# Moving a 32-byte constant to the front of its pool in a two-layer graph kernel on one NeuronCore

## The chip, the cores and the metric

The kernel runs on one core of one Trainium2 chip. The metric is device time in microseconds for one execution of the whole program. Before the change, three runs gave 1968.35, 1971.6 and 1975.02 us; the median is 1971.6 us.

## The reference, cut to what matters

The input is `x` with 128 batches of 128 rows by 512 features, and one 128x128 adjacency matrix `adj`. Two residual layers are applied, each followed by a layer norm.

```
# layer 0
A = adj @ x ;  C = adj @ x + b
y = max over features of relu(A_j + (C - A)_i)      # with equal weights this is relu(max_j A_j + b), one number per row
x = layernorm(x + y)
# layer 1: masked attention with 8 heads of 64
q, k, v = x @ w_qkv
p = softmax(where(adj == 0, -inf, q k^T / 8))
o = (p v) @ w_proj + b_proj
x = layernorm(x + o + layernorm(o) * gamma + beta)
```

## The kernel before, in words

The 128 batches are taken in 32 groups of four (`G = 4`). Within one group the matrix unit, TensorE, has these pieces of work:

- `conv` (line 186): `adj @ x` for one batch, in float32, with `adjT` as the stationary operand (the weights that are loaded into the array) and the batch's `xt` as the moving operand (the one that streams past). It feeds layer 0.
- `dense` (lines 342, 343 and 350): the q, k and v products of layer 1. To be fast and still exact enough, both factors are split into a high part, a low part and a difference, all kept in the type `fp32r`: `x_h`, `x_l`, `x_d` for the activations of a group and `w_h`, `w_l`, `w_d` for the weights. A product takes twelve matmuls of 128x128 against 512 columns: four slices of the inner dimension, each with the pairs of the high parts (342) and the low parts (343), and then four of the differences (350). The eight q and k products of a group have `w_*` stationary and `x_*` moving. The four v products have `x_*` stationary and `w_*` moving.
- `scores` (line 397) and `attend` (line 477): q times k, and v times the softmax weights, in float32, sixteen pairs of small matmuls a batch.
- `po` (function `project`, also lines 342, 343 and 350): the output projection, again twelve `fp32r` matmuls, with `p_h`, `p_l`, `p_d` moving and the split attention output `oh`, `ol`, `od` stationary. For the last eight batches (120 to 127) the split attention output is not put into `oh`, `ol`, `od`: the function `heads` writes it into slices of `w_h`, `w_l`, `w_d`, whose q and k columns are no longer needed by then. In the profile these projections are the ones that read `p_h,w_h` and so on.

The other engines feed this. VectorE (DVE) masks the scores, takes row maxima, scales the softmax weights and makes the low parts (lines 294 and 296). ScalarE (ACT) takes exponentials, norms and the high parts (line 303). GpSimd (POOL) makes the differences `x_d` and `od` (line 308) and prepares the residual `xb` (lines 500, 501 and 518; line 501 adds `beta_sb`). SyncE (SP) issues the transfers in a single queue, in order. Two of them are transposes through DRAM: the normalised batch (`xplanes` to `rowsx`, line 279, then `xT`, line 283) and the softmax weights (`planes` to `rows`, line 450, then `eT`, line 455).

The order on each engine is written out by a plan: a table of offsets `O` places each step relative to the matrix unit's estimated timeline, the steps are sorted by that place, and the order is then fixed (`tc.manual_schedule`).

SBUF memory is given out by pools, one after the other, in the order in which the pools are opened and, within a pool, in the order in which tiles are asked for; each tile takes a multiple of 32 bytes of every partition. The pool `const` comes first. It holds, in this order, `b0_sb` (4 bytes, padded to 32), `ident`, `adjT` and `mask` (512 bytes each), the six weight tensors `w_h` to `p_d`, `gamma_sb`, `bias_sb`, `beta_sb` (2,048 bytes each), the small constant `mhalf` (16 bytes, padded to 32; the exponent -0.5 that POOL uses at lines 241 and 536), and `square`. All large tensors of the pool have sizes that are multiples of 512 bytes. So the distance of a tensor from a multiple of 512 bytes (its address modulo 512) is set by what small tiles stand ahead of it:

| tensors | address modulo 512, before |
|---|---|
| `b0_sb` | 128 |
| `ident`, `adjT`, `mask`, `w_h` ... `p_d`, `gamma_sb`, `bias_sb`, `beta_sb`, `mhalf` | 160 |
| `square` and every large tile of the later pools: `xt`, `x_h`, `x_l`, `x_d`, `v`, `qkT`, `e`, `eT`, `o`, `xb`, `oh`, `ol`, `od` | 192 |

Of the kernel before, what the change touches and what calls it, by code (L numbers as in the profile page):

```python
# [8 lines left out]
FP = mybir.dt.float32  # L9
# [17 lines left out]
def tile_adj_resnorm_d2(  # L27
# [39 lines left out]
    P = 128  # L67
    assert T == P and D == 512 and B % 4 == 0
    G = 4
# [6 lines left out]
    const = ctx.enter_context(tc.tile_pool(name="const", bufs=1))  # L76
# [15 lines left out]
        xs[b] = xt  # L92


    adj_sb = work.tile([P, D], FP, tag="xh", name="adj_sb")[:, :P]
    nc.scalar.dma_start(adj_sb, adj)
    b0_sb = const.tile([P, 1], FP, name="b0_sb")
# [67 lines left out]
    gamma_sb = const.tile([P, D], FP, name="gamma_sb")  # L165
    bias_sb = const.tile([P, D], FP, name="bias_sb")
    beta_sb = const.tile([P, D], FP, name="beta_sb")
    mhalf = const.tile([P, G], FP, name="mhalf")
    nc.vector.memset(mhalf, -0.5)
    square = const.tile([P, D], mybir.dt.bfloat16, name="square")  # L170

# [727 lines left out]
```

## Time and profile before

| what | value |
|---|---|
| median of three runs | 1971.6 us (1968.35 to 1975.02) |
| profiled execution, span from the first to the last instruction | 1967.2 us |
| TensorE (PE) busy | 1872.0 us, 95% of the span |
| VectorE (DVE) busy | 1648.1 us, 84% |
| ScalarE (ACT) busy | 1547.6 us, 79% |
| GpSimd (POOL) busy | 1246.0 us, 63% |
| mean granted TensorE clock | 0.989 |

The profile shows one execution. Its page gives the span and no separate total for that execution; the span is 4.4 us under the median of the three runs, which also hold what lies around the first and the last instruction. A steady group takes about 58.9 us. A busy matrix unit in this profile is not one at its peak: the time of one matmul is best read from the distance between the starts of neighbours, since the ends are modelled.

### The profile page before, as it was taken

How to read it: one execution, taken by the hardware profiler on the slowest of the kernel's cores; microseconds unless marked ns; L12 is line 12 of the kernel's file. 1: busy time of each engine (PE TensorE's matmuls, PEld its weight loads, DVE VectorE, ACT ScalarE, POOL GpSimd, SP SyncE). 2: the span in 40 equal slices, each digit the busy share in tenths (PEclk: the TensorE clock that was granted, in tenths of full speed). 3: DMA queues.
4: the chain of work that ended last, by engine and by line, in shares of the span. 5: the costliest groups of instructions: out<-in, count | busy, mean ns of one | idle time of the engine just before them, and what ended most of it. 6: DMA issues, size and time to landing. Idle time of an engine off the chain costs nothing.

```text
span 1967.2 us, 33044 instructions
## 1 busy us (share of the span) xinstructions
PE 1872.0 (95%) x10569; PEld 1438.1 (73%) x10569; DVE 1648.1 (84%) x2585; ACT 1547.6 (79%) x3926; POOL 1246.0 (63%) x1935
## 2 busy tenths in 40 slices
PE   7799999999999999999999999999999999999995
PEld 4677777777777777777777777777777777777774
DVE  7778888888888888888888888888888888888875
ACT  4688878788878788878788878788878788878764
POOL 3256666666666666666666666666667666667667
PEclk9899999999999999999999999999999999999997
DMA  4366565666565666555666555766555666555641
GB/s 130 102 156 163 152 157 147 175 172 164 152 159 147 172 172 162 153 158 149 173 172 166 151 156 147 175 171 166 151 160 145 173 172 164 153 156 146 154 114 52
DMA packets 486141, 302.92 MB, mean 154 GB/s; under 512 B 399440, under 2 KB 403664, under 8 KB 485968
## 3 DMA queue, kind: packets, MB, share of 16 engines
q1 hardware_dynamic: 485104, 299.70, 57.2%
q8 instruction: 84, 1.38, 0.3%
q10 hardware_dynamic: 864, 1.12, 0.2%
q14 instruction: 89, 0.73, 0.1%
HBM read 72.16 MB, written 131.07 MB: 103 GB/s over the span
## 4 chain that ended last, share of the span: by engine, by line
PE 70%; POOL 11%; DVE 9%; issue 5%; ACT 3%; DMA 3%; SPq 0%; POOLq 0%; ACTq 0%; DVEq 0%
POOL x_d L308 5%; PE psc L397 5%; PE pav L477 5%; PE pa L186 3%; POOL od L308 2%; DMA eT<-rows 2%; DVE x_l L296 1%; DVE v L381 1%; POOL sum L536 1%; DVE xh L294 1%; ACT oh L303 1%; DVE o L523 1%; DVE o L548 1%; DVE o L509 1%; ACT x_h L303 1%
## 5 line engine op out<-in xcount | busy, mean ns | idle before, releaser
L431 ACT ACTIVATE e<-e,nmax 128x128 f32<-128x128 f32 x1016 | 393.1, 389 | 62.5 <-DVE nmax L422 62.5
L446 ACT COPY planes<-e 128x2048 uint16<-128x2048 uint16 x124 | 234.7, 1893 | 21.6 <-DVE e L440 21.5
L529 ACT ACTIVATE square<-o,sum 128x512 bf16<-128x512 f32 x256 | 183.1, 715 | 63.8 <-DVE o L523 62.8
L535 POOL TENSOR_SCALAR sum<-sum 128x1 f32<-128x1 f32 (+1 forms) x287 | 58.3, 203 | 269.8 <-ACT square L529 256.6
L501 POOL TENSOR_TENSOR xb<-xb,beta_sb 128x512 f32<-128x512 f32 x128 | 210.6, 1646 | 10.7
L308 POOL TENSOR_TENSOR x_d<-x_h,x_l 128x512 fp32r<-128x512 f32 x97 | 125.7, 1310 | 134.6 <-DVE x_l L296 74.9
L536 POOL TENSOR_TENSOR sum<-sum,mhalf 128x1 f32<-128x1 f32 (+1 forms) x287 | 181.1, 631 | 23.9
L431 ACT ACTIVATION_READ_ACCUMULATOR e<-e,nmax 128x1 f32 x1016 | 190.9, 188 | 0.0
L518 POOL TENSOR_TENSOR xb<-xb,o 128x512 f32<-128x512 f32 x125 | 164.6, 1317 | 4.9
L440 DVE TENSOR_TENSOR e<-e,sums 128x1024 f32<-128x1024 f32 x128 | 162.3, 1268 | 4.4
L548 DVE SCALAR_TENSOR_TENSOR o<-o,sum,gamma_sb 128x512 f32<-128x512 f32 x128 | 99.3, 776 | 76.5 <-POOL xb L518 72.9
L413 DVE SCALAR_TENSOR_TENSOR e<-psc,mask 128x1024 f32<-128x1024 f32 x127 | 151.8, 1216 | 3.3 <-ACT planes L446 2.7
L422 DVE TENSOR_REDUCE nmax<-e 128x8 f32<-128x1024 f32 x127 | 153.5, 1209 | 0.1
L477 PE MATMUL pav<-eT,v 128*64 128x128 f32 x2048 | 140.1, 280 | 11.4 <-DMA eT<-rows 5.4
L556 ACT ACTIVATE o<-o,sum 128x512 f32<-128x512 f32 x128 | 103.1, 807 | 54.6 <-POOL sum L544 54.6
L397 PE MATMUL psc<-qkT 64*128 64x128 f32 x2048 | 141.8, 284 | 2.5 <-DVE qkT L381 2.5
L500 POOL TENSOR_SCALAR xb<-xb,sum 128x512 f32<-128x512 f32 x128 | 120.8, 944 | 35.3 <-DMA xb<-in_x_dram 33.9
L397 PEld LDWEIGHTS psc<-qkT 64*128 64x128 f32 x2048 | 123.4, 189 | 25.9 <-issue 21.4
L259 ACT ACTIVATE xt<-xt,sum 128x512 f32<-128x512 f32 x127 | 102.4, 806 | 46.3 <-POOL sum L250 45.2
L477 PEld LDWEIGHTS pav<-eT,v 128*64 128x64 f32 x2048 | 110.8, 137 | 37.3 <-issue 15.4
L277 ACT COPY xplanes<-xt 128x1024 uint16<-128x1024 uint16 x124 | 129.7, 1046 | 5.1 <-DMA rowsx<-xplanes 1.2
L186 PE MATMUL pa<-xt,adjT 128*128 128x512 f32 x256 | 123.6, 607 | 6.9 <-ACT v L325 3.5
(4668 smaller groups left out, 5606.3 us busy)
## 6 DMA issues: line engine op xcount, KB each, us to landing
rows<-planes SPq DMA_DIRECT2D x124, 512.0 KB, 3.3
xt<-in_x_dram SPq DMA_DIRECT2D x128, 256.0 KB, 3.0
xb<-in_x_dram SPq DMA_DIRECT2D x128, 256.0 KB, 3.0
out_dram<-o SPq DMA_DIRECT2D x128, 256.0 KB, 2.8
rowsx<-xplanes SPq DMA_DIRECT2D x124, 256.0 KB, 2.4
wraw<-in_L_gnn_w_qkv_dram SPq DMA_DIRECT2D x8, 256.0 KB, 2.9
xT<-rowsx SPq DMA_TRANSPOSE x124, 3.6
eT<-rows SPq DMA_TRANSPOSE x124, 4.7
```

Source lines behind the costliest of these rows:

```text
L186: nc.tensor.matmul(pa[b], adjT, xs[b], start=True, stop=True)
L308: engine.tensor_tensor(fd, fh.bitcast(FP), fl.bitcast(FP), op=ALU.subtract)
L397: nc.tensor.matmul(psc[:, s, hp, :], qkT[hs, hp, i, :], qkT[hs, KC + hp, i, :], start=not with_mask, stop=not with_mask or hp == HP - 1,)
L422: nc.vector.tensor_reduce(nmax, src, AX.X, ALU.max, negate=True)
L431: nc.scalar.activation(e[:, j, :], src[:, j, :], AF.Exp, bias=nmax[:, j : j + 1], scale=1.0 if src is e else scale, accum_out=sums[:, j : ...
L440: nc.vector.tensor_tensor(e, e, sums[:, :, None].to_broadcast([P, H, P]), op=ALU.mult)
L446: nc.scalar.copy(planes, e.rearrange("p h m -> p (h m)").bitcast(U16).rearrange("p (m s) -> p s m", s=2),)
L477: nc.tensor.matmul(pavs[b][s * HD : (s + 1) * HD, hp, :], v[:, h * HD : (h + 1) * HD], eT[:, s * HP + hp, :], start=True, stop=True,)
L501: nc.gpsimd.tensor_tensor(xbs[b], xbs[b], beta_sb, op=ALU.add)
L518: engine.tensor_tensor(xbs[b], xbs[b], os[b], op=ALU.add)
L529: nc.scalar.activation(square, x, AF.Square, bias=s[:, 0:1], scale=-float(D), accum_out=s[:, 1:2],)
L536: nc.gpsimd.tensor_tensor(s, s, mhalf[:, :n], op=ALU.pow)
```

## The change

One line is moved and reworded. The tile `mhalf` is asked for at the start of the pool `const`, ahead of `b0_sb`, instead of after `beta_sb`. It is asked for with eight columns, of which a view takes the first four, so it takes 32 bytes in either place. The instructions that fill it (a memset on VectorE and a copy on ScalarE) stay where they were.

```diff
+    mhalf = const.tile([P, 8], FP, name="mhalf")[:, :G]
     adj_sb = work.tile([P, D], FP, tag="xh", name="adj_sb")[:, :P]
     nc.scalar.dma_start(adj_sb, adj)
     b0_sb = const.tile([P, 1], FP, name="b0_sb")
 ...
     beta_sb = const.tile([P, D], FP, name="beta_sb")
-    mhalf = const.tile([P, G], FP, name="mhalf")
     nc.vector.memset(mhalf, -0.5)
```

Every engine has the same instructions in the same order as before. What moves is memory: `mhalf` takes the place at 128, and `b0_sb`, `ident`, `adjT`, `mask`, the six weight tensors, `gamma_sb`, `bias_sb` and `beta_sb` lie 32 bytes further on. `square` and all later tiles keep their addresses. So the tensors at 160 modulo 512 go to 192, where the activations and split operands already are.

## The prediction

> **What bounds the kernel now.** I read the page first: busy shares, the slices over time and the chain that ended last.
>
> ```profile
> span 1967.2 us, 33044 instructions
> ...
> PE 1872.0 (95%) x10569; PEld 1438.1 (73%) x10569; DVE 1648.1 (84%) x2585; ACT 1547.6 (79%) x3926; POOL 1246.0 (63%) x1935
> ...
> PE   7799999999999999999999999999999999999995
> ...
> PE 70%; POOL 11%; DVE 9%; issue 5%; ACT 3%; DMA 3%; SPq 0%; POOLq 0%; ACTq 0%; DVEq 0%
> ```
>
> The matrix unit is busy in nine tenths or more of nearly every slice and holds 70% of the chain, so a change in the time of one matmul can move the end. No other engine is at its limit, but all of them touch the chain.
>
> Next I looked at what the change touches on the matrix unit. The fp32r products of q, k, v and of the projection have one operand in `w_*` or `p_*` (160 modulo 512) and the other in `x_*` or `o*` (192). The last eight batches are an exception that the kernel before holds by itself: there both operands lie in `p_*` and `w_*`, so both at 160. The timeline of PE (start, busy us, line, operands) has the two kinds side by side:
>
> ```profile
> 1892.13 0.40 PE L342 MATMUL pm_(31, 1)_19611<-w_h,x_h 128*128 128x512 f32 x1
> ...
> 1893.99 1.10 PE L350 MATMUL pd_(31, 1)_19612<-w_d,x_d 128*128 128x512 f32 x4
> 1894.93 0.39 PE L342 MATMUL pm_('o', 120)_19626<-p_h,w_h 128*128 128x512 f32 x1
> ...
> 1896.74 1.07 PE L350 MATMUL pd_('o', 120)_19627<-p_d,w_d 128*128 128x512 f32 x4
> ...
> 1950.87 0.39 PE L342 MATMUL pp_('o', 126)_20088<-p_h,w_h 128*128 128x512 f32 x1
> ...
> 1952.68 1.07 PE L350 MATMUL pp_('o', 126)_20088<-p_d,w_d 128*128 128x512 f32 x4
> ```
>
> Eight matmuls lie between a first start and its line 350. Operands at unlike distances: 1893.99 - 1892.13 = 1.86 us, 232.5 ns each; with the next four, 1894.93 - 1892.13 = 2.80 us, 233.3 ns each over twelve. Like distances, immediately afterwards: 1896.74 - 1894.93 = 1.81 us, 226 ns each, and again 1.81 us at 1950.87. Instruction, shape and clock are the same, and the other engines' work is that of the same microseconds. Start by start, the unlike kind alternates between 231 and 235 ns, the like kind between 226 and 227.
>
> Last, the chain of waits over one steady group (start, us, what), to see which matmuls lie on it:
>
> ```profile
> 1023.38 0.25 PE pm_(16, 3)_10517 L343
> 1023.62 0.02 issue
> 1023.64 2.55 POOL x_d L308 x2
> ...
> 1029.56 1.30 POOL x_d L308
> 1030.86 1.42 POOL od L308
> 1032.28 0.04 issue
> 1032.32 1.20 PE pd_('o', 63)_10606 L350 x4
> ```
>
> From 1023.6 to 1032.3 the chain runs through POOL, while the matrix unit does the projection of batch 62, two convs and most of batch 63, and then waits 1.0 us for `od`. Everything else in the group, 1000.0 to 1058.9, is matmul after matmul.
>
> [...]
>
> **The change part by part.** It removes and adds no instruction, transfer or wait and moves no queue: the memset and the copy that fill `mhalf` keep their places. What it moves is the second operand.
>
> Number of matmuls: lines 342, 343 and 350 have 2,040 each, 6,120 in all. The projections of batches 120 to 127 (8 x 12 = 96) already have like distances, before and after. So 6,024 go from unlike to like.
>
> Price of one: 233.3 - 226.6 = 6.7 ns in a settled stream. But a like stream is not always settled from its first matmul. Batch 120 is; batches 121, 123 and 127 need six to ten matmuls after a pause at some 231 ns, and batch 124, which is broken up by a wait, does not settle. A steady group has 16 products of 12, which makes 192 fp32r matmuls, in about six streams, each begun after small matmuls or a wait. Eight slow ones each are 48 that win about 2 ns, and 144 win 6.7: 0.10 + 0.96 = 1.06 us a group, 5.5 ns a matmul. All 6,024 settled would be 40 us of PE time over the kernel; at 5.5 ns it is 33 us.
>
> What lies on the path: in the group shown, 12 matmuls of batch 62 and 8 of batch 63 lie beside POOL's stretch, so 172 of 192 are on the chain. The sum over the chain's pieces on these three lines is 1,141 us, or about 4,890 matmuls of 233.3 ns. They bound the gain: 4,890 x 6.7 = 33 us if all settle, 27 us at 5.5 ns. No faster matmul can bring more unless it settles below 226.
>
> What is late next: the softmax weights of the fourth batch of a group.
>
> ```profile
> 1011.42 0.34 SPq L279 DMA_DIRECT2D rowsx<-xplanes  x1
> 1011.86 2.13 SPq L455 DMA_TRANSPOSE eT<-rows  x1
> ...
> eT<-rows SPq DMA_TRANSPOSE x124, 4.7
> ```
>
> The queue's timeline and the page's transfer list: issued at 1011.86 behind `rowsx`, which waits for ScalarE's `xplanes` (line 277), and landed some 4.7 us later, at about 1016.5. The attend of that batch starts at 1016.56. Eleven times in the kernel PE is seen idle for it, 5.4 us in all. So the two v products and two projections ahead of it, 48 matmuls, run beside an equally long path through ScalarE, and what they win is lost in that wait unless ScalarE's work has come forward too. That leaves 172 - 48 = 124 matmuls a group: 124 x 5.5 = 0.68 us, times 31 groups, 21 us. With the 48 counted it is 29 us. I take 21, because the landing is that close in every group.
>
> Other engines: VectorE, ScalarE and POOL read `mask`, `gamma_sb`, `bias_sb` and `beta_sb` at the new place. I cost this at nothing. POOL's line 501 (`xb` at 192 with `beta_sb` at 160) has a mean of 1,646 ns against 1,317 for line 518 with both at 192, which could look like placement. But single ones of line 501 take 1.30 us (at 1899.57 in the chain), as line 518 does[...]. From both sides: if all of the difference were placement, POOL would gain 128 x 0.33 = 42 us of busy time, of which the chain holds six pieces of line 501, so 2 us; a loss is limited likewise.
>
> Sum: the span of 1967.2 becomes about 1946; against the median of the runs, 4.4 us above that span, 1971.6 - 21 = 1950.6, said as 1951.
>
> **The rivals.**
> 1. The gain is swallowed: each wait for `eT` and `od` grows by what PE wins. For it: `eT` lands as it is needed. Against: the chain goes through that transfer only eleven times, and the 72 matmuls of six q and k products in a row have no such partner. It would give 1961 to 1971.
> 2. The change doesn't do what it says: the quick projections are quick because both operands sit at 160, or because of which tensors they are, and 192 with 192 is like any other pair. Against: five of the projections reach 226 to 227 with weights at different multiples of 512. It gives 1971.6.
> 3. Slower: at a common distance of 192 the weight load and the moving read get into each other's way in every fp32r matmul. Place: the same 4,890 on the chain; price: as much as the gain, 6.7 ns, so 1971.6 + 33 = 2004; it decides from 1.2 ns a matmul (4,890 x 1.2 = 5.9 us). Against: the float32 scores have both operands in `qkT`, at 192, and the prologue's v products have both at 192 and take 429 ns an instruction, as the conv with unlike operands does.
> 4. More than forecast: all streams settle and ScalarE's path comes forward with them, 1971.6 - 33 = 1938, or lower if 192 is better than 160.
>
> **How the numbers follow.** The forecast, 14 to 34 us less, has 0.66; a larger gain 0.05; rival 1 has 0.17, most of it still over the bound; rival 2 has 0.05, rival 3 0.07. A measurement of this kernel can tell about 0.3%, 5.9 us, from no change. So faster has 0.84, same 0.09, slower 0.07. The range of 1937 to 1967 takes the settled bound at its low end and the weaker part of rival 1 at its high end.
>
> **What would show it.** Right: twelve fp32r matmuls of q, k and v in 2.72 to 2.77 us where there were 2.80, steps of 226 to 227 ns in the long q and k stretch, conv and scores unchanged, a steady group near 58.2 us, and longer waits of the fourth attend for `eT`. Wrong: steps that remain at 231 and 235 (rival 2) or go above (rival 3); or steps of 227 with a group of 58.9 us (rival 1).

## The result and the profile after

The changed kernel takes 1975.5 us (median of four runs, 1971.05 to 1979.84) against 1970.3 us for the kernel before beside it: a ratio of 1.0029 with a 95% interval of 1.0007 to 1.0051. It is no faster, but slower by some 5 us. The forecast of 1951 us, with a range of 1937 to 1967, was wrong.

The page of the changed kernel, for the execution of 1971.05 us:

```profile
span 1969.2 us, 33044 instructions
...
PE 1844.8 (94%) x10569; PEld 1438.0 (73%) x10569; DVE 1671.3 (85%) x2585; ACT 1550.6 (79%) x3926; POOL 1273.3 (65%) x1935
...
PE   7799999999999999999999999999999999999995
...
PE 59%; POOL 14%; DVE 9%; ACT 7%; issue 5%; DMA 5%; POOLq 0%; ACTq 0%; SPq 0%; DVEq 0%
```

PE works 27.2 us less than before (1872.0 - 1844.8) in a span that is 2 us longer, and its share of the chain falls from 70% to 59%. Two other engines, which execute the same instructions in the same order, are busier: VectorE by 23 us, POOL by 27 us. The granted clock is the same (0.988 after, 0.989 before).

The matmuls did what was forecast. The timeline of PE has three streams of twelve, one after the other:

```profile
1005.85 0.39 PE L342 MATMUL pm_('o', 60)_10338<-p_h,oh 128*128 128x512 f32 x1
...
1008.57 0.39 PE L342 MATMUL pm_(16, 1)_10370<-w_h,x_h 128*128 128x512 f32 x1
...
1011.29 0.39 PE L342 MATMUL pm_('o', 61)_10405<-p_h,oh 128*128 128x512 f32 x1
```

Twelve take 2.72 us, 227 ns each, where they took 2.80 us. Over the kernel the mean distance of neighbouring starts (pauses of 250 ns and more left out) went from 233.3 to 227.8 ns for q and k, and from 233.2 to 228.5 ns for v and the projections. Yet the median period of a steady group is 58.92 us, where it was 58.90. What PE won reappears as idle time ahead of the attend. The waits of PE (total us, times, longest us), where before had 5.4, 11 and 0.9:

```profile
PE pav L477 <- DMA eT<-rows: 28.7, 26, 2.6
```

The tempting reading is that the transfer of `eT` was tied with PE all along and has swallowed the gain. The other half of the profile speaks against stopping there. These are groups of instructions on the page (busy us, mean ns, idle before):

```profile
L518 POOL TENSOR_TENSOR xb<-xb,o 128x512 f32<-128x512 f32 x125 | 175.2, 1401 | 4.9
...
L523 DVE SCALAR_TENSOR_TENSOR o<-o,sum,xb 128x512 f32<-128x512 f32 x128 | 132.5, 1035 | 10.8 <-POOL sum L536 0.9
```

The same groups before, from the list of all groups:

```profile
L518 POOL TENSOR_TENSOR xb<-xb,o 128x512 f32<-128x512 f32 x125 | 164.6, 1317 | 4.9
...
L523 DVE SCALAR_TENSOR_TENSOR o<-o,sum,xb 128x512 f32<-128x512 f32 x128 | 112.6, 880 | 10.8 <-POOL sum L536 0.9 <-POOL sum L541 0.5
```

The timelines show where the difference comes from. First the kernel before, VectorE and POOL between 954 and 963 us, in a steady group:

```profile
954.67 0.69 DVE L509 SCALAR_TENSOR_TENSOR o<-pm_('o', 57)_9783,bias_sb 128x512 f32<-128x512 f32 x1 [0.98 <-PE pm_('o', 57)_9783 L343]
...
957.33 0.19 POOL L535 TENSOR_SCALAR sum<-sum 128x1 f32<-128x1 f32 x1 [0.76 <-ACT square L529]
...
958.27 1.51 POOL L301 TENSOR_SCALAR x_h<-xh 128x512 fp32r<-128x512 f32 x1
...
958.58 1.39 DVE L440 TENSOR_TENSOR e<-e,sums 128x1024 f32<-128x1024 f32 x1
959.87 1.30 POOL L518 TENSOR_TENSOR xb<-xb,o 128x512 f32<-128x512 f32 x1
...
962.13 0.75 DVE L523 SCALAR_TENSOR_TENSOR o<-o,sum,xb 128x512 f32<-128x512 f32 x1
```

Then the changed kernel, the same instructions of the same group:

```profile
954.40 0.69 DVE L509 SCALAR_TENSOR_TENSOR o<-pm_('o', 57)_9783,bias_sb 128x512 f32<-128x512 f32 x1 [0.84 <-PE pm_('o', 57)_9783 L343]
...
957.76 0.19 POOL L535 TENSOR_SCALAR sum<-sum 128x1 f32<-128x1 f32 x1 [1.33 <-ACT square L529]
...
958.46 1.23 DVE L440 TENSOR_TENSOR e<-e,sums 128x1024 f32<-128x1024 f32 x1
958.70 2.35 POOL L301 TENSOR_SCALAR x_h<-xh 128x512 fp32r<-128x512 f32 x1
...
961.13 1.76 POOL L518 TENSOR_TENSOR xb<-xb,o 128x512 f32<-128x512 f32 x1
961.85 1.59 DVE L523 SCALAR_TENSOR_TENSOR o<-o,sum,xb 128x512 f32<-128x512 f32 x1
```

Before, POOL starts its line 301 at 958.27, 0.31 us ahead of VectorE's line 440, both go on nearly undisturbed (1.51 and 1.39 us; in the group at 132.09 us, where line 301 starts 0.56 us ahead, 1.51 and 1.23), and POOL is through with line 518 at 961.17, before VectorE comes to line 523. After, line 440 starts first. The matmuls hand VectorE its input 0.27 us earlier (its line 509 starts at 954.40 instead of 954.67), while POOL is later: it waits until 957.76 instead of 957.33 for ScalarE's `square`, which stands in a backlog that ran 0.43 us later from its first copy on (line 277 at 951.87 instead of 951.44). Set against line 509, this first copy has moved by 0.70 us: it starts 2.53 us ahead of it instead of 3.23. Line 301 now takes 2.35 us, line 518 slides behind it, and line 523 meets line 518 and takes 1.59 us instead of 0.75. I call this the **meeting**. Of 26 steady groups it is there in all 26 after the change (line 523 takes over 1.2 us), and in 3 before.

From the start of line 509 (projection of a group's second batch) to the end of the fourth batch's line 413, VectorE needs 11.03 us before and 11.85 us after (medians over the groups; the idle time in it is 0.32 us in both). This is **VectorE's stretch** below. What follows is 0.8 us later for it, counted from line 509: `od` starts 8.97 us behind it instead of 8.14, POOL's `x_d` 10.89 instead of 10.07. That the delay goes on from there through ScalarE's backlog and `rowsx` in SP's queue to `eT` is argued from what depends on what; where it costs time is for the experiments to show.

In the two timelines, which pass starts first decides what VectorE loses. With POOL's line 301 ahead it is 0.16 us, on line 440 (1.39 us against 1.23). With line 440 ahead, line 301 takes 2.35 us instead of 1.51, and VectorE loses 0.84 us later, on line 523, which starts 0.72 us after line 518 (1.59 against 0.75). That passes of the two engines lengthen each other is measured; what they contend for is not shown.

### The profile page after: what moved, and what is told of

It reads as the page before. It is cut to its first block, busy times and chain, and to the rows that moved or that the text cites. A ratio compares the mean times of both kernels' runs of the same rounds, so it can differ in the third digit from the quotient of the medians.

```text
span 1969.2 us, 33044 instructions
## 1 busy us (share of the span) xinstructions
PE 1844.8 (94%) x10569; PEld 1438.0 (73%) x10569; DVE 1671.3 (85%) x2585; ACT 1550.6 (79%) x3926; POOL 1273.3 (65%) x1935
## 4 chain that ended last, share of the span: by engine, by line
PE 59%; POOL 14%; DVE 9%; ACT 7%; issue 5%; DMA 5%; POOLq 0%; ACTq 0%; SPq 0%; DVEq 0%
POOL x_d L308 5%; PE pav L477 4%; PE psc L397 4%; DMA eT<-rows 3%; PE pa L186 2%; POOL od L308 2%; ACT e L431 2%; POOL sum L536 2%; POOL xb L501 1%; DVE x_l L296 1%; DVE v L381 1%; DVE xh L294 1%; POOL xb L518 1%; POOL xb L500 1%; DVE o L523 1%
## 5 line engine op out<-in xcount | busy, mean ns | idle before, releaser
L518 POOL TENSOR_TENSOR xb<-xb,o 128x512 f32<-128x512 f32 x125 | 175.2, 1401 | 4.9
L440 DVE TENSOR_TENSOR e<-e,sums 128x1024 f32<-128x1024 f32 x128 | 157.7, 1232 | 4.4
L523 DVE SCALAR_TENSOR_TENSOR o<-o,sum,xb 128x512 f32<-128x512 f32 x128 | 132.5, 1035 | 10.8 <-POOL sum L536 0.9
```

The source lines that it names most:

```text
L440: nc.vector.tensor_tensor(e, e, sums[:, :, None].to_broadcast([P, H, P]), op=ALU.mult)
L518: engine.tensor_tensor(xbs[b], xbs[b], os[b], op=ALU.add)
L523: nc.vector.scalar_tensor_tensor(os[b], in0, scalar, in1, op0=ALU.mult, op1=ALU.add, accum_out=s[:, 0:1],)
```

## The experiments

Eighteen runs. The expectations name their theories themselves. In short, the theories are: the late `eT` in SP's queue eats the gain; the new place of `mask`, `gamma_sb`, `bias_sb` and `beta_sb` costs another engine time; PE and a second loop through POOL, ScalarE and SP are tied; and the meeting of VectorE and POOL. Every ratio is to the kernel before, on the same chip. A group is the median period over 26 steady groups of the profiled run.

### Getting `eT` out of SP's queue

The order on SP is set by due times. An early due time puts `eT` ahead of both `rowsx` transfers:

```diff
-'softmax': {'cross': [-11.04, -10.0, -15.2, -5.92],
+'softmax': {'cross': [-11.04, -10.0, -15.2, -40.0],
```

`b_early` is this in the kernel before, `a_early` in the changed one.

> The kernel before with one entry of the plan changed: the transfer of the softmax weights (eT) of the fourth batch of each group stands earlier in SP's queue, ahead of two rowsx transfers. Theory 1 (two loops of equal length, 58.9 us a group: one of matmuls, one through POOL, VectorE, ScalarE and SP that ends in this eT): the matmul loop is as long as before, so 1964 to 1972 us, and the idle time of PE ahead of attend for eT falls from 5.4 us to under 2. Theory 2 (the moved vectors slow VectorE and POOL): says nothing of this run beyond the same.

> The changed kernel with the same entry of the plan: eT of the fourth batch earlier in SP's queue. Theory 1: the wait of 28.7 us for eT goes to under 5, the 27 us of shorter matmuls show, and the time is 1945 to 1958 us, 14 us or more under the kernel before with the same entry. Theory 2 (the new place of mask, gamma, beta and bias slows VectorE and POOL and so sets the end): 1968 to 1976 us, no better than the changed kernel.

Measured: 2001.3 us (ratio 1.0152, 1.0126 to 1.0177) and 2000.1 us (1.0141, 1.0114 to 1.0168), a group of 59.9 and 59.8 us. The wait for `eT` is gone, but both times lie far above what every theory gave: this edit has a cost of its own. With it PE waits for `v` instead, probably because `rowsx` and the `xT` behind it, on which `v` depends, now come late. The waits of PE in `a_early`:

```profile
PE pav L477 <- ACT v L377: 17.1, 22, 1.8
```

Besides, the meeting is present in both (line 523 at 1.58 us), in the kernel before too. So the pair tells nothing of the gain. A milder due time puts `eT` ahead of one `rowsx` only, into a gap of SP's queue:

```diff
-'softmax': {'cross': [-11.04, -10.0, -15.2, -5.92],
+'softmax': {'cross': [-11.04, -10.0, -15.2, -8.5],
```

`a_c85` is this in the changed kernel, `b_c85` in the kernel before.

> The changed kernel with the eT of the fourth batch ahead of only one rowsx transfer, in a gap of 3.1 us that SP's queue has there. Theory 1 (the end is set by a loop without fp32r matmuls, which closes through this eT): the wait of 28.7 us for eT goes to under 6, no other transfer is held up by more than 1 us, and the gain of the matmuls shows: 1945 to 1962 us. Theory 2 (the new place of mask, gamma, beta and bias slows VectorE and POOL): 1968 to 1976 us. Theory 3 (several loops of nearly the same length, so that taking one away brings the next): 1960 to 1972 us with another wait of 15 us or more on PE.

> The kernel before with the same entry of the plan. Theory 1: the matmul loop is the only one left, 58.8 us a group: 1962 to 1971 us, with under 2 us of waits for eT. Theory 3: as much or slower, 1966 to 1976 us.

Measured: 1971.9 us (0.9998, 0.9989 to 1.0006) and 1969.5 us (0.9983, 0.9975 to 0.9992). In `a_c85` PE no longer waits for `eT`, and nothing is won: a group still takes 58.94 us. The wait moved to the first matmul of a projection. PE's timeline of `a_c85`, with the idle time ahead and its releaser in brackets:

```profile
971.02 0.50 PE L342 MATMUL pp_('o', 58)_9921<-p_h,oh 128*128 128x512 f32 x1 [1.29 <-DVE e L413]
```

The idle time of PE ahead of a projection that ends with VectorE's line 413, the end of VectorE's stretch, rose from 6.1 us in the changed kernel to 39.6 (between 120 and 1880 us; in `b_c85` it is 14.9). So the late `eT` was where most of the loss showed, not where it arose. The time alone would also fit the theory of the vectors' new place; the next pair tests that.

### The place of the vectors against the place of the weights

`w_only` has the six weight tensors alone at 192 (the three vectors and `mhalf` are asked for ahead of `w_h`), `v_only` has `ident`, `adjT`, `mask` and the vectors at 192 and the weights at 160.

```diff
 # w_only: ahead of w_h
+    gamma_sb = const.tile([P, D], FP, name="gamma_sb")
+    bias_sb = const.tile([P, D], FP, name="bias_sb")
+    beta_sb = const.tile([P, D], FP, name="beta_sb")
+    mhalf = const.tile([P, G], FP, name="mhalf")
```

```diff
 # v_only: the weights w_h ... p_d, then mhalf, ahead of ident
+    mhalf = const.tile([P, G], FP, name="mhalf")
     ident = const.tile([P, P], FP, name="ident")
```

> The six weight tensors alone at 192 modulo 512; ident, adjT, mask, gamma, bias and beta stay at 160. Theory 1: like the changed kernel, matmuls of 227 to 228 ns, 25 us or more of waits for eT, 1968 to 1977 us. Theory 2: matmuls of 227 to 228 ns, and the time 1940 to 1958 us, since the vectors have their old place.

> The other half alone: ident, adjT, mask, gamma, bias and beta at 192, the weight tensors at 160. Theory 1: like the kernel before, matmuls of 233 ns, VectorE's line of o<-o,sum,xb at 880 ns as before, 1966 to 1974 us. Theory 2: matmuls of 233 ns, VectorE's o<-o,sum,xb at 1,035 ns as in the changed kernel, and over 1980 us.

Measured: `w_only` 1979.5 us (1.0027, 1.0010 to 1.0044; 2.5 us above what theory 1 gave), matmuls at 227.8 to 228.4 ns, meeting present (stretch 11.86 us). `v_only` 1974.2 us (1.0005, 0.9996 to 1.0014), matmuls at 233.2 ns, no meeting (11.03 us). The place of the vectors is out as a cause: the faster matmuls bring the meeting with them.

### POOL with less to do

`b_nobeta` and `a_nobeta` leave out line 501 (`beta_sb` is not added to the residual).

```diff
-        nc.gpsimd.tensor_tensor(xbs[b], xbs[b], beta_sb, op=ALU.add)
```

> The kernel before without line 501: beta (zeros here) is not added to the residual, which takes 128 instructions of 1.65 us off POOL. Theory 1: the loop through POOL gets some 3 us a group shorter, the matmul loop stays 58.8 us, so the time falls by little: 1960 to 1970 us. Theory 2: the same.

> The changed kernel without line 501 (beta, zeros here, is not added). Theory 1: with the loop through POOL shorter, the matmul loop with its 5.5 ns less a matmul sets the end: 1940 to 1956 us, 14 us or more under the kernel before without that line, and the idle time of PE for eT is under 8 us. Theory 2: the two kernels without that line differ by less than 6 us, the changed one not faster.

Measured: 1966.8 us (0.9980, 0.9968 to 0.9991) and 1960.6 us (0.9946, 0.9925 to 0.9967): 6 us of the gain appear, where theory 1 asked for 14 or more. POOL's load is part of the loop, but line 523 still takes 1.58 us in `a_nobeta` (stretch 11.65) and 0.75 in `b_nobeta` (11.02), so the meeting was still there.

### Taking the meeting away

In `a_h0` and `b_h0` ScalarE (line 303) instead of POOL (line 301) makes `x_h` of a group's first batch. `a_h0c85` and `b_h0c85` have the due time -8.5 as well.

```diff
-         'h': [1, 0, 0, 0, 0, 1, 0, 0],
+         'h': [0, 0, 0, 0, 0, 1, 0, 0],
```

> The changed kernel with one entry of the allotment altered: x_h of the first batch of a group is made by ScalarE (L303) instead of GpSimd (L301), so GpSimd's L301 no longer runs beside VectorE's L440 and L518 no longer slides onto L523. Collision theory (most of the gain is eaten by VectorE and GpSimd meeting there, 0.8 us a group): L523 back at 0.75 us, the stretch from L509 to the end of L413 of the fourth batch back near 11.0 us, the wait for eT ahead of the fourth attend down by half or more, and the time 6 to 20 us under the same alteration without the change (b_h0): 1950 to 1966 us. Tied-loop theory (a second path of 58.8 us a group through SP's rowsx and eT has almost no fp32r matmuls in it, so the gain can't show whatever the collision costs): L523 back at 0.75 us, but the period stays at 58.7 to 58.9 us and PE's wait at 0.8 us or more a group: 1964 to 1976 us.

> The kernel before with x_h of the first batch of a group made by ScalarE (L303) instead of GpSimd (L301). Both theories: nothing much, 1962 to 1975 us, since VectorE and GpSimd did not meet there before; ScalarE gets one more pass of some 0.6 us a group, which could make its backlog ahead of rowsx later. L523 stays at 0.75 us.

> The changed kernel with both alterations: x_h of the first batch by ScalarE, and the eT transfer issued ahead of one of rowsx's (due time of 'cross' -8.5), so that neither the collision nor SP's queue stands in the way. Collision theory: the first matmul of po no longer waits for VectorE's e (L413), 0.8 us a group less: group 57.9 to 58.3 us, 1940 to 1960 us. Tied-loop theory: with the queue out of the way the tie is broken too, but the loop behind it, ScalarE's backlog and VectorE's e, is what po's first matmul waits for: 1962 to 1974 us.

> The kernel before with both alterations. Both theories: 1958 to 1972 us; the difference to a_h0c85 is what the faster matmuls are worth with both obstacles gone: 15 to 28 us by the collision theory, under 8 us by the tied-loop theory.

Measured:

| kernel | median us | ratio (interval) | VectorE's stretch us | group us |
|---|---|---|---|---|
| `a_h0` | 1965.1 | 0.9954 (0.9938 to 0.9970) | 11.02 | 58.39 |
| `b_h0` | 1990.1 | 1.0091 (1.0072 to 1.0110) | 11.90 | 59.72 |
| `a_h0c85` | 1950.6 | 0.9891 (0.9870 to 0.9913) | 11.03 | 58.09 |
| `b_h0c85` | 1988.4 | 1.0086 (1.0066 to 1.0105) | 11.91 | 59.74 |

`a_h0` came out within what the theory of the meeting gave, at the weak end, and one part of it was missed: the wait for `eT` did not halve, it rose to 36.1 us. So there is something in the tie as well; with the queue out of the way (`a_h0c85`) the rest of the gain appears. VectorE and POOL still meet in `a_h0`, but VectorE's line 440 starts 0.13 us ahead of line 518 (median), and it is POOL that pays, 2.23 us for line 518. `b_h0` and `b_h0c85` were misses of both theories, which had put them near the kernel before: they are 0.9% slower. The timeline of `b_h0` shows why:

```profile
967.39 1.28 POOL L518 TENSOR_TENSOR xb<-xb,o 128x512 f32<-128x512 f32 x1 [0.31 <-DVE o L523]
967.47 2.29 DVE L440 TENSOR_TENSOR e<-e,sums 128x1024 f32<-128x1024 f32 x1
```

Without line 301 ahead of it, POOL's line 518 starts 0.08 us before VectorE's line 440, which then takes 2.29 us instead of 1.39. This made the next pair.

### Only the order of two neighbours

`a_swap` and `b_swap` exchange lines 301 and 518 on POOL in each group; each instruction stays on its engine, and no other queue changes. `a_swapc85` has the due time -8.5 as well.

```diff
- 'x_high': [-2.23, 2.47, -9.83, 1.18],
+ 'x_high': [1.77, 2.47, -9.83, 1.18],
```

> The changed kernel with one due time altered ('x_high'[0] from -2.23 to 1.77): in each group two neighbours on GpSimd change places, L518 (xb<-xb,o) then L301 (x_h<-xh) instead of L301 then L518; every instruction stays on its engine. Collision theory (what costs 0.8 us a group is which of VectorE's and GpSimd's passes starts first): VectorE's L440 starts ahead of L518 and keeps 1.23 us, L518 takes 2.2 us beside it, L523 is back at 0.75 to 0.95 us, the stretch from L509 to the end of L413 back at 11.0 to 11.3 us, and the time 8 to 16 us under the changed kernel: 1958 to 1968 us. Theory that the collision is a symptom (VectorE isn't what the path waits for, and moving x_h to ScalarE helped by relieving GpSimd): as the changed kernel, 1970 to 1977 us.

> The kernel before with the same two neighbours on GpSimd exchanged. Collision theory: here GpSimd is ready 0.3 us before VectorE, so L518 starts ahead of L440, which then takes 2.2 to 2.3 us instead of 1.39: the stretch grows by 0.7 to 0.9 us, and the time to 1982 to 1992 us. The same exchange that makes the changed kernel faster makes this one slower. Theory that the collision is a symptom: no difference, 1966 to 1974 us.

> The changed kernel with the exchange on GpSimd and the eT transfer ahead of one of rowsx's (due time of 'cross' -8.5). Both obstacles gone with no work moved to another engine. Collision theory with the tied loops: a group of 57.9 to 58.2 us and 1942 to 1956 us. If the gain of a_h0c85 came from ScalarE's taking over x_h: 1964 to 1972 us.

Measured: `a_swap` 1964.2 us (0.9965, 0.9951 to 0.9978), `b_swap` 1987.6 us (1.0081, 1.0067 to 1.0095), `a_swapc85` 1958.6 us (0.9933, 0.9914 to 0.9952; 3 us above what was expected). The same exchange makes the changed kernel faster and the kernel before slower. The timeline of `a_swap`:

```profile
960.19 1.23 DVE L440 TENSOR_TENSOR e<-e,sums 128x1024 f32<-128x1024 f32 x1
960.33 2.23 POOL L518 TENSOR_TENSOR xb<-xb,o 128x512 f32<-128x512 f32 x1
...
962.74 1.05 DVE L548 SCALAR_TENSOR_TENSOR o<-o,sum,gamma_sb 128x512 f32<-128x512 f32 x1
963.91 0.75 DVE L523 SCALAR_TENSOR_TENSOR o<-o,sum,xb 128x512 f32<-128x512 f32 x1
```

And of `b_swap`:

```profile
969.30 1.27 POOL L518 TENSOR_TENSOR xb<-xb,o 128x512 f32<-128x512 f32 x1 [0.24 <-DVE o L523]
969.37 2.28 DVE L440 TENSOR_TENSOR e<-e,sums 128x1024 f32<-128x1024 f32 x1
...
973.83 0.75 DVE L523 SCALAR_TENSOR_TENSOR o<-o,sum,xb 128x512 f32<-128x512 f32 x1
```

With VectorE 0.14 us ahead, POOL pays (2.23 us instead of about 1.3) and VectorE's line 440 keeps its 1.23 us; with POOL 0.07 us ahead, POOL's pass takes 1.27 us and VectorE's line 440 takes 2.28 us. In `a_swap` line 548, beside the displaced line 301, gives 0.3 us back (1.05 instead of 0.74), which is why its stretch is 11.41 and not 11.03 us.

With `eT` out of the way, the length of VectorE's stretch can be set against the group. "Like" are kernels with weights and split operands at the same place modulo 512, "unlike" those with 160 and 192:

| distances | kernel | stretch us | group us |
|---|---|---|---|
| like | `a_h0c85` | 11.03 | 58.09 |
| like | `a_swapc85` | 11.44 | 58.49 |
| like | `a_c85` | 11.88 | 58.94 |
| unlike | `b_c85` | 11.03 | 58.87 |
| unlike | `b_h0c85` | 11.91 | 59.74 |

Among the first three the group grows by 0.40 and 0.45 us where the stretch grows by 0.41 and 0.44: one for one. PE's timeline shows the same steps as the wait for line 413. `a_swapc85`:

```profile
964.89 0.50 PE L342 MATMUL pp_('o', 58)_9921<-p_h,oh 128*128 128x512 f32 x1 [0.80 <-DVE e L413]
```

`a_h0c85`:

```profile
957.97 0.50 PE L342 MATMUL pp_('o', 58)_9921<-p_h,oh 128*128 128x512 f32 x1 [0.45 <-DVE e L413]
```

That is 1.29, 0.80 and 0.45 us. At an equal stretch, like distances bring 58.87 - 58.09 = 0.78 us a group with the short one, and 59.74 - 58.94 = 0.80 us with the long one. `a_h0c85` is the fastest version: 1.1% under the kernel before, by the faster matmuls, `x_h` on ScalarE and the earlier `eT` together.

The same kernels tell which way the cause runs. ScalarE's first copy of the backlog (line 277) starts 3.23 us ahead of line 509 in `b_c85`, with the short stretch, and in `b_h0c85`, with the long one; it starts 2.51 us ahead in `a_h0c85`, with the short stretch, and 2.49 us in `a_c85`, with the long one (medians over the 26 groups). So the shift of 0.7 us goes with the faster matmuls and is not an effect of the longer stretch.

### Is it the likeness, and of what unit?

`s160` puts `mhalf` into the tile of `b0_sb` in the kernel before, so that weights and split operands both lie at 160. `a_pad64` and `a_pad256` put a tile of 64 or 256 bytes at the end of `const` in the changed kernel, so that the weights stay at 192 and the split operands go to 256 or 448.

```diff
 # s160
-    b0_sb = const.tile([P, 1], FP, name="b0_sb")
+    front = const.tile([P, 8], FP, name="front")
+    b0_sb, mhalf = front[:, :1], front[:, 4:8]
```

```diff
 # a_pad64 ([P, 64] in a_pad256)
+    pad_sb = const.tile([P, 16], FP, name="pad_sb")
+    nc.vector.memset(pad_sb, 0.0)
```

> The kernel before with mhalf put into b0's tile, 32 bytes of each partition in all: weights and split operands both begin 160 bytes past a multiple of 512 (changed kernel: both at 192; before: 160 and 192). If it is the likeness that makes the matmuls faster: 226 to 227 ns from start to start, mean 228. If it is the place 192 itself: 232 to 233 ns.

> The changed kernel with 64 bytes more in each partition behind the constants' pool (a memset of 128x16 is added ahead of the loops): weights at 192 as in the changed kernel, split operands at 256, so they are 64 bytes apart modulo 512. If what counts is that the distances are equal modulo 512: 232 to 233 ns from start to start, as before. If only the place within 64 bytes counts (before they differed by 32): 226 to 227 ns.

> The same with 256 bytes more (a memset of 128x64): weights at 192, split operands at 448, 256 bytes apart modulo 512. If 512 bytes are the unit: 232 to 233 ns. If the unit is 256 bytes or less: 226 to 227 ns.

Measured, as the mean distance of starts: `s160` 227.8 (q and k), 228.5 (v) and 228.3 ns (projection), so the likeness counts and not the place 192. `a_pad64` 229.3, 233.3 and 233.3 ns; `a_pad256` 227.7, 228.5 and 228.5 ns. The last is a miss for a unit of 512 bytes: operands 256 bytes apart are as quick as operands at the same place. PE's timeline of `a_pad64` (two lines were added to this kernel, so line 342 is 344):

```profile
1013.11 0.40 PE L344 MATMUL pm_('o', 60)_10340<-p_h,oh 128*128 128x512 f32 x1
...
1015.91 0.40 PE L344 MATMUL pm_(16, 1)_10372<-w_h,x_h 128*128 128x512 f32 x1
```

And of `a_pad256`:

```profile
1007.25 0.39 PE L344 MATMUL pm_('o', 60)_10340<-p_h,oh 128*128 128x512 f32 x1
...
1009.97 0.39 PE L344 MATMUL pm_(16, 1)_10372<-w_h,x_h 128*128 128x512 f32 x1
```

Twelve in 2.80 us at 64 bytes apart, and in 2.72 us at 256. Single times of 1977.1 us (`s160`), 1977.6 (`a_pad64`) and 1972.7 (`a_pad256`) say nothing finer of the whole; the meeting was there in all three (line 523 at 1.58 us). In `a_pad64` a part of the gain is enough for it: the projections are as slow as before and only q and k gain some 4 ns a matmul, yet line 301 starts 0.04 us after line 440 (median), and 21 of the 26 groups have the meeting.

## Why the prediction was wrong, point by point

**The price of a matmul was right.** The forecast took 6.7 ns in a settled stream and 5.5 ns on the mean. Measured were 5.5 ns for q and k and 4.7 ns for v and the projections; for the 33 us of PE time that were forecast, PE's busy time fell by 27.2. Conv, scores and attends kept their times (606, 285 and 280 ns a matmul, where before had 607, 284 and 280).

**What lies on the path was counted about right, but only where `eT` is out of the way.** The forecast put 1.06 us a group at most on the path and kept 0.68 us after leaving out 48 matmuls. The pairs of equal stretch show 0.78 and 0.80 us, and their measured times, by the ratios, are 18 and 17 us apart, where 21 were forecast. With `eT` left in SP's queue, as in the forecast kernel, less comes through even when VectorE is spared: `a_h0` is 9 us under the kernel before and `a_swap` 7, again by the ratios. The median group of `a_h0` is 0.51 us shorter (58.90 - 58.39), but single groups wait up to 2.3 us for `eT`, and the mean group is only 0.27 us shorter. Both kernels carry an alteration of their own, so how much of the 21 us the queue alone takes is not settled; the deduction for `eT` looks too small rather than too large.

**The step that failed is "Other engines", costed at nothing.** It asked only whether the new place of the vectors costs something (`v_only`: it doesn't). It did not ask what a faster PE does to the order in which VectorE and POOL start. That shifts by some 0.5 us in all (line 440 0.12 us earlier, line 301 0.43 us later), turns a lead of 0.31 us for POOL into one of 0.24 us for VectorE, and lengthens VectorE's stretch by 0.82 us a group. In kernels with unlike distances such a stretch means a group of 59.75 us (`b_swap`) instead of 58.90, and a time 16 us longer (1.0081). That is about what the faster matmuls win, 17 to 18 us: with `eT` out of the way the changed kernel is level with the kernel before (`a_c85`, 0.9998). With `eT` in its old place it is 5.2 us slower (1.0029). This rest goes with that transfer: in the profile of the changed kernel single groups wait up to 2.6 us for `eT`, so that its mean period rose by 0.14 us where the median rose by 0.02 (in `a_c85` the mean is 0.03 above the kernel before). Why just these groups wait so long is open.

**Rival 1** foresaw the picture (steps of 227, a group of 58.9 us, longer waits for `eT`) and not the cause. Its two waits did not both grow: `od` went from 29.3 to 30.5 us only. And with a tie through the queued `eT` alone `a_c85` would have been fast. As a bound it was also too kind, since it had no way to end above the kernel before. **Rival 2** is refuted by the steps, **rival 3** too (nothing rose above 233 ns). The forecast's 0.07 for a slower kernel stood wholly on rival 3, which no run showed; what came, a neighbour's pass that begins too early, was missing from the list.

## What to carry to other kernels

When one engine gets faster, its consumers can start earlier (here line 509 by 0.27 us), and the passes of two other engines may change places: read the start times of VectorE's and GpSimd's passes next to each other, and where they are close, treat the order as part of the forecast; here a lead of 0.31 us did not last, and line 523 went from 0.75 to 1.59 us. A new wait on the fast engine tells where a delay arrives; to find where it arises, compare the durations of identical instructions in both traces first. Then mend that meeting (an exchange of two neighbours, or one pass on another engine) before judging the change itself.

## What the runs showed that was not expected

- The fp32r matmuls of 128x128 against 512 columns stepped at 233 ns with their operands at 160 and 192 modulo 512 (the kernel before, `v_only`), and at 227 ns in settled streams, 227.7 to 228.5 on the mean, with 160 and 160 (`s160`), 192 and 192 (the changed kernel) and 192 and 448 (`a_pad256`): in these runs, at the same place modulo 256. A distance of 128 was not tried, so the unit may be smaller. With the weights at 192 and the split operands at 256 (`a_pad64`), it mattered which operand was which: v and the projections, where the weights are the moving operand, stayed at 233 ns, while q and k, where they are the stationary one, averaged 229 ns. Other distances were not tried, and the reason is open.
- Where passes of VectorE and GpSimd with two inputs each started 0.07 to 0.14 us apart, the one that started later took about as much longer as the other still needed: in `b_swap` line 440, 0.07 us behind line 518 with 1.20 us left, took 2.28 us instead of 1.23; in `a_swap` line 518, 0.14 us behind line 440 with 1.09 us left, took 2.23 us instead of 1.3. GpSimd's one-input pass, line 301, was milder when it was first than when it was second: behind it VectorE lost 0.16 us at a lead of 0.31 us, and 0.38 us in one group of the kernel before where the lead was 0.09 us (at 781.64 us, line 440 at 1.61 us), while as the second it lost 0.84 us itself.
